# Making the last layers' weights once, ahead of the scans, and loading them for the third batch from another queue

## The chip, the cores and the metric

The kernel runs on one core of one Trainium2 chip. The metric is the device time of one execution in microseconds (us); lower is better. The core's engines run beside each other, each through its own list of instructions in order: TensorE (PE in the profile, PEld for its weight loads), VectorE (DVE), ScalarE (ACT), GpSimd (POOL) and SyncE (SP), which here only issues DMAs. They wait for each other on semaphores. ACT and POOL can issue DMAs too.

## The reference, cut to what matters

The input has four batches of 384 channels by 32 by 32 positions. Two layers follow one another, each a mixer and a feed-forward part with a residual around it:

```python
# layer 0: a selective scan in four directions, then a mixture of experts
x = x + _L0_conv_ref(_ln_c(x), ...)          # scan over 1024 positions, 16 states, 4 directions
t = t + _L0_ffn_ref(_ln_t(t), ...)           # 4 experts, the 2 best for each token
# layer 1: attention with 8 heads, then a feed-forward part with Kronecker weights
x = x + _L1_conv_ref(_ln_c(x), ...)          # out = einsum('bne,ce->bnc', out, w_out) + b_out
t = t + _L1_ffn_ref(_ln_t(t), ...)

def _L1_ffn_ref(x, c_fc_1, c_fc_2, c_proj_1, c_proj_2):
    w_fc = jnp.kron(c_fc_1, c_fc_2)          # (1536, 32) by (1, 12): 1536 by 384
    w_proj = jnp.kron(c_proj_1, c_proj_2)
    h = jax.nn.gelu(x @ w_fc.T, approximate=False)
    return h @ w_proj.T
```

The "last layers" are attention's output projection (`w_out`), the layer norm of tokens behind it, and `_L1_ffn_ref`. The norm's mean can be worked into the first weight (each value of `c_fc_2` less the mean of its row over the 384 columns), and `c_proj_2` into the last one. Both are what the change is about. These weights are the same for all batches.

## The kernel before, in words

**Tiling.** A batch is 384 channels by 1024 positions: three chunks of 128 partitions, two halves of 512 columns. The scans (`scan_layer`) run over 32 units: four batches, four directions, two halves. In each unit `chunk` runs over three chunks of channels and four groups of states. Its work on the engines: POOL multiplies (L445 and L473, `bx`), ACT takes exponentials (L454, `da`), DVE scans (L459) and multiplies (L466), and PE sums over states (L480, `acc`). SP issues the loads of the scan's operands (`dtr` L429, `bcs` L355), which `project` has written to DRAM as `dd` (L410, L411) and `both`.

**The tail of a batch.** When the scan of batch b is done, `between(b)` emits `tail_batch(b - 1)`: the experts of that batch, then attention, then `last_layers`. So a tail is interleaved with the scan of a later batch: the first batch's last layers lie near 1600 us, beside the end of the second batch's scan, and the second batch's near 2550, beside the start of the fourth's. The third batch's lie near 3510, just after all scans, and the fourth's near 4106, with nothing beside them. The fourth batch's experts begin right after the third batch's attention; their weights (`w`, 576 KB each, L927 and L935, loaded by SP in `fetch`) go into a second set of buffers (the `Room` called "w", with ten `kw` buffers) that is free only after the scans.

**Attention** (`attention`) works over four pairs of heads t, two halves i and eight blocks j. PE makes scores (L1146, `s_ps`), ACT their exponentials (L1152, `ex`), and PE the weighted sum (L1195, `o_acc`), which ACT copies to `att` once for each half (L1203). Then `divide` sums the rows on DVE (L1160, `inv`), takes the reciprocal there (L1161), spreads it by PE (L1168, `bc_ps`) and multiplies on DVE (L1173).

**The last layers** (`last_layers`) load three tiles: `wa` (576 KB, three quarters of `w_out`, L1219), `wb` (384 KB: the last quarter of `w_out`, and the mean-free first weight `wz`, L1221) and `wc` (576 KB: `fc1`, `pj1` and `pj2`, L1223). DVE then subtracts the mean from `wz` in place (L1225) and multiplies `pj2` by `c_proj_2` (L1230). PE projects attention's output (L1248, `o_ps`, which takes `wa` and, for the last quarter, `wb`), and so on to the output. All three tiles have the tag `kw`, whose eight buffers (`NARROW`) they share with attention's own tiles and with expert weights.

**What sets the order.** The kernel is one program of tiles without an order written by hand. `build` opens it with `schedule_with_timeline_sim=True`: a planner lays out each engine's list by its own estimate of when operations become ready, with priorities. `last_layers` is emitted under `high_priority(offset=FORWARD)`, so that its operations come ahead of others when they are ready. Operations that need nothing late, such as those of `moe_consts`, are laid out near the start of the kernel, although the code calls them in the first tail. Once laid out, an engine's list is fixed, and an instruction that waits holds everything behind it on its engine.

**The queues.** All loads and stores shown here are issued by SP, except the two first loads (`cols` L128, `wx` L199) and the first gather of each batch's tokens (`xs`, L952, for s equal to 0), which ACT issues, and the scatters and gathers by index (L697, L1044), which POOL issues.

Of the kernel before, what the change touches and what calls it, by code (L numbers as in the profile page):

```python
# [9 lines left out]
F32 = mybir.dt.float32  # L10
I32 = mybir.dt.int32
AF = mybir.ActivationFunctionType
ALU = mybir.AluOpType
# [4 lines left out]
P = 128  # L18
B = 4
D = 384  # L20
# [40 lines left out]
KR = 32  # L61
KJ = D // KR
# [12 lines left out]
COL = {}  # L75
# [42 lines left out]
class Body:  # L118
# [436 lines left out]
    def moe_consts(self, room):  # L555
        nc, a, wp = self.nc, self.a, self.const


        turn = wp.tile([P, DC, P + NE], F32, tag="turn", name="turn")
        wg = turn[:, :, P:]  # L560
        nc.sync.dma_start(out=wg, in_=a["wg"].rearrange("(c p) e -> p c e", p=P))
        for c in range(DC):
            nc.vector.tensor_copy(turn[:, c, :P], self.ident)
        ps = room.bank("p", "wg_ps")
        for c in range(DC):
            nc.tensor.matmul(ps[:, :NE], self.ones, wg[:, c, :], start=(c == 0), stop=(c == DC - 1))
        for c in range(DC):
            nc.vector.scalar_tensor_tensor(
                wg[:, c, :], ps[:, :NE], -1.0 / D, wg[:, c, :], op0=ALU.mult, op1=ALU.add
            )  # L570
        self.turn = turn
        bg = wp.tile([P, NE], F32, tag="bg", name="bg")
        nc.sync.dma_start(out=bg, in_=a["bg"].partition_broadcast(P))
        self.bg = bg

        def count(name, shape, pattern, base=0, channel=0):
            i = wp.tile([P, *shape], I32, tag=name, name=name + "_i")
            nc.gpsimd.iota(i, pattern=pattern, base=base, channel_multiplier=channel)
            f = i.bitcast(F32)
            nc.vector.tensor_copy(f, i)  # L580
            return f


        before = count("before", [P], [[1, P]], channel=-1)
        nc.vector.tensor_scalar(before, before, 0.0, None, op0=ALU.is_gt)
        self.before = before
        lower = count("lower", [NE, NE], [[1, NE], [-1, NE]])
        nc.vector.tensor_scalar(lower, lower, 0.0, None, op0=ALU.is_gt)
        self.lower = lower
        self.full = count("full", [L // P], [[P, L // P]])  # L590
        self.slot_at = count("slot_at", [NSLOT], [[1, NSLOT]])
        self.number = count("number", [MB], [[P, MB]], base=1, channel=1)
        self.column = count("column", [P], [[1, P]], base=1)


        size = NROW
        self.rows = self.dram.tile([size, W], F32, tag="rows", name="rows")
        self.made, self.zeroed, self.taken = [], [], []
        for b in range(B):
            self.made.append(self.dram.tile([STORED, D], F32, tag=f"made{b}", name=f"made{b}"))  # L600
# [607 lines left out]
    def last_layers(self, b, att, room, between=()):  # L1208
# [4 lines left out]
        nc, a = self.nc, self.a  # L1213
        nq = P // KR
        nt = INNER // P


        wa = room.tile([P, nt - 1, D], "kw", "wa")
        nc.sync.dma_start(out=wa, in_=a["wa"].rearrange("p (t d) -> p t d", d=D))  # L1219
        wb = room.tile([P, 2, D], "kw", "wb")  # L1220
        nc.sync.dma_start(out=wb, in_=a["wb"].rearrange("p (t d) -> p t d", d=D))  # L1221
        wc = room.tile([P, 3, D], "kw", "wc")
        nc.sync.dma_start(out=wc, in_=a["wc"].rearrange("p (t d) -> p t d", d=D))  # L1223
        wz = wb[:, 1, :]
        nc.vector.tensor_scalar(wz, wz, self.c2mean, None, op0=ALU.subtract)  # L1225
        fc1 = wc[:, 0, :].rearrange("p (q m) -> p q m", m=P)
        pj1 = wc[:, 1, :].rearrange("p (f r) -> p f r", r=KR)
        pj2 = wc[:, 2, :]
        lo, hi = COL["pj2"]
        nc.vector.tensor_mul(  # L1230
            pj2.rearrange("p (r j) -> p r j", j=KJ), pj2.rearrange("p (r j) -> p r j", j=KJ),
            self.cols[:, lo:hi].unsqueeze(1).to_broadcast([P, KR, KJ]),
        )

        x2 = [room.tile([P, L], "kw", "x2") for _ in range(DC)]
        zt = room.tile([P, NH, HF], "k4", "z")
# [1 line left out]
        for i in range(NH):  # L1238
            part = []
# [3 lines left out]
            for c in range(DC):  # L1243
                ps = room.bank("p", "o_ps")
                chunk = slice(c * P, (c + 1) * P)
                for t in range(nt):
                    w = wa[:, t, chunk] if t < nt - 1 else wb[:, 0, chunk]
# [73 lines left out]
        for i in range(NH):  # L1321
            out = room.bank("p" if between and i == 0 else "o", "f_acc")
# [252 lines left out]
```

## Time and profile before

| | us |
|---|---|
| median of 3 runs | 4209.68 |
| lowest and highest of the runs | 4201.19 and 4214.02 |
| the profiled execution's own time | 4199.62 |
| its span in the profile | 4197.9 |

| engine | busy us | share of the span | instructions |
|---|---|---|---|
| PE | 3348.0 | 80% | 13372 |
| PEld | 1574.9 | 38% | 13372 |
| DVE | 2872.9 | 68% | 4250 |
| ACT | 2463.8 | 59% | 4485 |
| POOL | 3022.8 | 72% | 1476 |

The mean clock granted to TensorE is 0.877 of full speed. The profile is of one execution; times in it count from the start of its span. Busy shares are averages over stages with different limits, so what a change is worth has to be read in its stage: by windows (busy time of each engine between two times), by timelines (the instructions of one engine in order, with the idle time before each and who ended it), and by waits (who waited for whom). A name such as `bx<-dtr,bcs` means that tile `bx` is written from `dtr` and `bcs`. A line such as L445 is a line of the kernel; SPq and ACTq are DMAs that SP and ACT issue, and their length is that of the issue and not of the transfer.

### The profile page before, as it was taken

Reading aid. Unit: us, or ns where it says so; the run is one execution under the profiler, and the core shown is the slowest. Engines: PE = TensorE matmul, PEld = TensorE weight load, DVE = VectorE, ACT = ScalarE, POOL = GpSimd, SP = SyncE. Lnnn points to the kernel's source line nnn. Section 1 sums busy time; section 2 is a strip of 40 time slices with the busy share of each in tenths; the row PEclk is TensorE's granted clock in tenths of the full one; section 3 lists DMA queues with packets and bytes.
Section 4 is the critical chain, followed back from the end, with each engine's and each line's share of the span. In section 5 each row is a group of like instructions: output and inputs, shape, how many; then the busy total and the mean of one; then the engine's idle time right before and its main releaser. Section 6 shows DMA issues by size and latency. Waiting matters only on the chain. (4 is left out here: it accounts for less than half of the span.)

```text
span 4197.9 us, 45862 instructions
## 1 busy us (share of the span) xinstructions
PE 3348.0 (80%) x13372; PEld 1574.9 (38%) x13372; DVE 2872.9 (68%) x4250; ACT 2463.8 (59%) x4485; POOL 3022.8 (72%) x1476
## 2 busy tenths in 40 slices
PE   6545454479987888789996887789996988999899
PEld 2101111145553223255553223245563224577423
DVE  5999997878887877788887867788887862010101
ACT  5555555556665776776665776676665774421353
POOL 5999997898989877798989976888998961000100
PEclk8666666589998999799998998789998999999999
DMA  5554464577986444577886434568887424356200
GB/s 139 126 136 124 111 176 111 154 226 217 254 249 179 103 131 120 170 213 228 233 252 192 112 105 137 153 195 241 224 249 220 109 64 170 122 179 208 88 6 31
DMA packets 378883, 677.67 MB, mean 161 GB/s; under 512 B 49920, under 2 KB 179328, under 8 KB 378624
## 3 DMA queue, kind: packets, MB, share of 16 engines
q1 hardware_dynamic: 368800, 647.42, 54.1%
q0 software_dynamic: 8192, 25.21, 1.9%
q8 instruction: 108, 1.77, 0.2%
q10 hardware_dynamic: 1632, 2.04, 0.2%
q14 instruction: 151, 1.24, 0.1%
HBM read 566.68 MB, written 107.79 MB: 161 GB/s over the span
## 5 line engine op out<-in xcount | busy, mean ns | idle before, releaser
L445 POOL TENSOR_TENSOR bx<-dtr,bcs 128x1024 f32<-128x1024 f32 x768 | 1795.4, 2365 | 189.1 <-PE acc L480 103.1
L454 ACT ACTIVATE da<-dtr,nega 128x512 f32<-128x512 f32 x1536 | 1044.5, 690 | 921.1 <-DVE bx L466 568.3
L473 POOL TENSOR_TENSOR bx<-bx,bcs 128x1024 f32<-128x1024 f32 x384 | 907.2, 2366 | 138.3 <-DVE carry L470 69.2
L480 PE MATMUL acc<-bx,sel 128*32 128x512 f32 x3072 | 495.4, 707 | 320.8 <-POOL bx L473 294.6
L991 PE MATMUL h_ps<-xc,w 128*128 128x256 f32 (+1 forms) x3168 | 652.3, 361 | 45.6 <-DMA w<-in_w 18.4
L1013 PE MATMUL y_ps<-w,hs 128*128 128x384 f32 x1824 | 630.2, 497 | 26.9 <-ACT hs L1004 18.7
L991 PEld LDWEIGHTS h_ps<-xc,w 128*128 128x128 f32 x3168 | 547.4, 196 | 202.4 <-issue 87.0
L459 DVE TENSOR_TENSOR_SCAN bx<-da,carry,bx 128x512 f32<-128x512 f32 x384 | 474.1, 1270 | 118.2 <-POOL bx L445 64.8
L459 DVE TENSOR_TENSOR_SCAN da<-da,carry,bx 128x512 f32<-128x512 f32 x384 | 475.9, 1273 | 77.6 <-ACT da L454 68.7
L459 DVE TENSOR_TENSOR_SCAN bx<-da,bx 128x512 f32<-128x512 f32 x384 | 451.9, 1210 | 95.1 <-POOL bx L445 54.7
L466 DVE TENSOR_TENSOR bx<-da,bcs 128x512 f32<-128x512 f32 x768 | 509.4, 680 | 3.9 <-DMA bcs<-both 0.4
L459 DVE TENSOR_TENSOR_SCAN da<-da,bx 128x512 f32<-128x512 f32 x384 | 455.2, 1218 | 68.8 <-ACT da L454 55.5
L1013 PEld LDWEIGHTS y_ps<-w,hs 128*128 128x128 f32 x1824 | 345.1, 193 | 305.3 <-issue 56.1
L1146 PE MATMUL s_ps<-w 64*128 64x512 f32 x1024 | 311.2, 663 | 76.6 <-ACT ex L1152 72.2
L1152 ACT ACTIVATE ex<-s_ps 128x512 f32<-128x512 f32 x512 | 300.7, 591 | 107.3 <-PE s_ps L1146 105.7
L1044 POOL DMA_INDIRECT got<-made,g_source x64 | 61.2, 957 | 401.1 <-PE h_ps L991 381.4
L999 ACT ACTIVATE hs<-h_ps,bb 128x256 f32<-128x256 f32 (+1 forms) x528 | 200.4, 441 | 240.5 <-PE h_ps L991 178.5
L1195 PE MATMUL o_acc<-ex,vt 128*64 128x512 f32 x1024 | 287.5, 639 | 23.2 <-ACT ex L1152 20.8
L480 PEld LDWEIGHTS acc<-bx,sel 128*32 128x32 f32 x3072 | 73.9, 116 | 611.2 <-POOL bx L473 404.8
L1146 PEld LDWEIGHTS s_ps<-w 64*128 64x128 f32 x1024 | 83.6, 190 | 287.3 <-ACT ex L1152 235.7
L370 PE MATMUL dt_ps<-xd,wdt 108*128 108x512 f32 x192 | 124.7, 736 | 59.5 <-ACT mag L409 30.5
L1017 DVE TENSOR_TENSOR y<-y_ps,bb 128x384 f32<-128x384 f32 x76 | 41.7, 549 | 170.0 <-PE y_ps L1013 170.0
(240 smaller groups left out, 3594.2 us busy)
## 6 DMA issues: line engine op xcount, KB each, us to landing
w<-in_w SPq DMA_DIRECT2D x352, 576.0 KB
dtr<-dd SPq DMA_DIRECT2D x1536, 128.0 KB
bcs<-both SPq DMA_DIRECT2D x512, 128.0 KB
dd<-one_e SPq DMA_DIRECT2D x96, 256.0 KB
dd<-mag SPq DMA_DIRECT2D x96, 256.0 KB
xt<-x SPq DMA_DIRECT2D x32, 384.0 KB
made<-y SPq DMA_DIRECT2D x32, 384.0 KB
xs<-rows SPq DMA_DIRECT2D x28, 385.0 KB
```

Source lines behind the costliest of these rows:

```text
L445: pool = nc.gpsimd.tensor_mul(bx, dtr[q][1], bc[:, 0].unsqueeze(1).to_broadcast([P, 2, HF])).ins
L454: nc.scalar.activation(da, dtr[q][0][:, j, :], AF.Exp, scale=nega[:, col : col + 1])
L459: nc.vector.tensor_tensor_scan(run(h), run(da), run(bx[:, j, :]), 0.0 if first else hold, ALU.mult, ALU.add,)
L466: dve = nc.vector.tensor_mul(bx[:, j, :], h, cg).ins
L473: pool = nc.gpsimd.tensor_mul(bx, bx, cg.unsqueeze(1).to_broadcast([P, 2, HF])).ins
L480: nc.tensor.matmul(acc[lo : lo + DB, :], sel, out[q][:, j, :], start=(g == 0), stop=(g == NG - 1),)
L991: ins = nc.tensor.matmul(ps[:, r, :], w1[(f + r) // wf][:, c, (f + r) % wf * P : ((f + r) % wf + 1) * P], xc[:, c, :], start=(c == 0), sto ...
L999: done = nc.scalar.activation(hs[:, f + r, :], ps[:, r, :], AF.Gelu if last or alone else AF.Identity, bias=bb[:, f + r : f + r + 1],).ins
L1013: nc.tensor.matmul(out[:, :D], hs[:, f, t * P : (t + 1) * P], w2[f // wf][:, f % wf, :], start=(f == 0), stop=(f == FC - 1),)
L1146: ins = nc.tensor.matmul(ps, w[rows, j * P : (j + 1) * P], w[rows, halves(i)], start=True, stop=True).ins
L1152: done.append(nc.scalar.activation(ex[:, o, :], ps, AF.Exp, scale=HD**-0.5, accum_out=sums[:, t, 2 * j + o, i : i + 1],).ins)
L1195: ins = nc.tensor.matmul(out[cols, :], made[t][1][:, j, cols], ex[:, o, :], start=(j == 0), stop=(j == MB - 1),).ins
```

## The change

`wb` and `wc` are no longer loaded raw and finished by DVE in each batch. In `moe_consts` they are loaded once, by ACT's queue, into two `kw` buffers; DVE subtracts the mean and multiplies by `c_proj_2` there; and ACT's queue stores the finished tiles to two tiles in DRAM. `last_layers` loads from those. Its three loads are issued by SP as before in batches 0, 1 and 3, and by ACT in batch 2, the third. The two DVE operations in `last_layers` are gone. `wa` still comes straight from the input.

```diff
@@ moe_consts
+        self.weights = []
+        for name, n in (("wb", 2), ("wc", 3)):
+            w = room.tile([P, n, D], "kw", name)
+            nc.scalar.dma_start(out=w, in_=a[name].rearrange("p (t d) -> p t d", d=D))
+            part = w[:, n - 1, :]
+            if name == "wb":
+                nc.vector.tensor_scalar(part, part, self.c2mean, None, op0=ALU.subtract)
+            else:
+                lo, hi = COL["pj2"]
+                part = part.rearrange("p (r j) -> p r j", j=KJ)
+                nc.vector.tensor_mul(
+                    part, part, self.cols[:, lo:hi].unsqueeze(1).to_broadcast([P, KR, KJ])
+                )
+            ready = self.dram.tile([P, n, D], F32, tag=name, name=name)
+            nc.scalar.dma_start(out=ready, in_=w)
+            self.weights.append(ready)
@@ last_layers
+        queue = nc.scalar if b == B - 2 else nc.sync
         wa = room.tile([P, nt - 1, D], "kw", "wa")
-        nc.sync.dma_start(out=wa, in_=a["wa"].rearrange("p (t d) -> p t d", d=D))
+        queue.dma_start(out=wa, in_=a["wa"].rearrange("p (t d) -> p t d", d=D))
         wb = room.tile([P, 2, D], "kw", "wb")
-        nc.sync.dma_start(out=wb, in_=a["wb"].rearrange("p (t d) -> p t d", d=D))
+        queue.dma_start(out=wb, in_=self.weights[0])
         wc = room.tile([P, 3, D], "kw", "wc")
-        nc.sync.dma_start(out=wc, in_=a["wc"].rearrange("p (t d) -> p t d", d=D))
+        queue.dma_start(out=wc, in_=self.weights[1])
         wz = wb[:, 1, :]
-        nc.vector.tensor_scalar(wz, wz, self.c2mean, None, op0=ALU.subtract)
...
-        lo, hi = COL["pj2"]
-        nc.vector.tensor_mul(
-            pj2.rearrange("p (r j) -> p r j", j=KJ), pj2.rearrange("p (r j) -> p r j", j=KJ),
-            self.cols[:, lo:hi].unsqueeze(1).to_broadcast([P, KR, KJ]),
-        )
```

## The prediction

> **What bounds the kernel now.** I read the table of slices, then windows by stage, then what waits inside the stages that the edit touches (timelines of one engine each, and the queue's waits). Windows first; columns are stretch, length, then PE, PEld, DVE, ACT, POOL busy (instructions), granted clock, DMA share, GB/s.
>
> ```profile
> 1640.10:1798.60 158.50, 119.68 (x414) 45.38 (x413) 111.16 (x238) 106.34 (x159) 121.02 (x68) 0.80 0.53 158
> 2545.20:2702.00 156.80, 118.10 (x444) 48.73 (x442) 113.77 (x231) 90.93 (x164) 108.23 (x63) 0.83 0.51 157
> ...
> 2702.00:3428.00 726.00, 627.07 (x2629) 317.54 (x2631) 597.62 (x809) 490.69 (x851) 653.99 (x311) 0.91 0.67 187
> ...
> 3522.00:3900.00 378.00, 378.00 (x1576) 256.73 (x1575) 34.62 (x65) 104.91 (x192) 6.70 (x7) 0.99 0.49 160
> ```
>
> During the scans (44 to 3428 us) POOL is the fullest engine, 654 of 726 in the third row, with DVE just behind and feeding it. The exceptions are the first units of a batch's scan: in the first unit of the fourth batch (second row) POOL works 108.2 of 156.8. From 3522 to 3900 TensorE is full. So a stop of DVE counts in the scans, a stop of PE counts after them. The last layers stand in both.
>
> The second batch's DVE and POOL timelines (start, length, engine, line, operation, idle before and who ended it):
>
> ```profile
> 2545.14 0.27 DVE L470 COPY carry<-bx 128x1 f32<-128x1 f32 x2
> 2549.86 10.64 DVE L1225 TENSOR_SCALAR wb<-wb,c2mean 128x384 f32<-128x384 f32 x1 [4.45 <-DMA wb<-in_wb]
> 2560.42 2.33 DVE L459 TENSOR_TENSOR_SCAN da<-da,bx 128x512 f32<-128x512 f32 x2
> ```
> ```profile
> 2551.03 9.26 POOL L445 TENSOR_TENSOR bx<-dtr,bcs 128x1024 f32<-128x1024 f32 x4
> 2568.89 2.34 POOL L473 TENSOR_TENSOR bx<-bx,bcs 128x1024 f32<-128x1024 f32 x1 [8.61 <-DVE carry L470]
> 2576.69 2.35 POOL L473 TENSOR_TENSOR bx<-bx,bcs 128x1024 f32<-128x1024 f32 x1 [5.45 <-DVE carry L470]
> ```
>
> An operation that takes 0.41 us when POOL is idle (fourth batch, 4073.43) stood 10.64 us here, until POOL's row of products ended at 2560.3; with the wait for its weights before it, DVE did nothing else for 15.1 us. POOL ran ahead on its buffers, then stood 8.6 and 5.5 us.
>
> The third batch, PE, then DVE, then SP's queue:
>
> ```profile
> 3509.11 1.08 PE L1195 MATMUL o_acc<-ex,vt 128*64 128x512 f32 x4 [0.34 <-ACT ex L1152]
> 3521.79 2.39 PE L1168 MATMUL bc_ps<-ident,inv 128*64 128x128 f32 x18 [11.60 <-DVE inv L1161]
> ```
> ```profile
> 3520.97 0.42 DVE L1225 TENSOR_SCALAR wb<-wb,c2mean 128x384 f32<-128x384 f32 x1 [11.69 <-DMA wb<-in_wb]
> 3521.50 0.24 DVE L1161 RECIPROCAL inv<-inv 128x16 f32<-128x16 f32 x1
> ```
> ```profile
> 3493.21 3.69 SPq L935 DMA_DIRECT2D w<-in_w  x4
> 3499.49 4.78 SPq L927 DMA_DIRECT2D w<-in_w  x2
> 3505.60 0.35 SPq L1219 DMA_DIRECT2D wa<-in_wa  x1
> 3508.43 2.69 SPq L1221 DMA_DIRECT2D wb<-in_wb  x1
> 3511.25 0.35 SPq L1223 DMA_DIRECT2D wc<-in_wc  x1
> ```
> ```profile
> SPq L1219 <- DMA w<-in_w: 1.3, 1, 1.3
> ```
>
> PE idles 11.6 us because the reciprocal is queued on DVE behind L1225, which waits for wb, which SP issued behind ten loads of expert weights. The last row matters too: the load of wa waited for an earlier load to land. The operands in the trace show eight completion semaphores that DMAs of SP and ACT take in turn, so each load waits until the load eight before it has landed. SP could go on at 3505.6, 3508.4 and 3511.2.
>
> **The change, part by part.** The sum is made against the profiled execution, 4199.6 us, 10.1 under the median 4209.7.
>
> Removed in all: four L1225 (13.3 us busy, 22.2 idle before) and four L1230 (2.6 and 0.5), 38.6 us of DVE. That is the ceiling without the queue's move; what counts is less.
>
> First batch: DVE stood from 1595.8 to 1603.7, but its next scan needs a product that POOL ended at 1601.2. Gain 2.4 us, plus some of L1230's 0.9: 2.5 (0 to 4).
>
> Second batch: the next scan's product (L445, 2545.16, 2.37 us) was ready at 2547.5, and the scan began at 2560.4: 12.9 us. POOL's two stalls behind it sum to 14.1, and ACT waited 12.9 in one piece for DVE. I take 12.5 (4 to 15). The Trainium skill speaks here, in "SBUF — State Buffer", section "Who interferes with whom": DVE's two-port modes and GpSimd exclude each other, and whoever issues first holds the port pair for that instruction. By it L1225 loses at most the POOL product under way, 2.4 us, so the stop would be 4.5 + 2.4 + 0.4 = 7.3 and the gain some 5. The row shows four and a half products passing first. The row is used; by the rule the sum below would be 7.5 us worse.
>
> Third batch, DVE: PE's 11.6 us wait for the reciprocal goes, less the 0.5 that the reduction and the reciprocal take themselves: gain 11.1. Next late would be wa (landed 3519) for o_ps, if it stayed on SP.
>
> Third batch, the queue: three loads leave SP and stand in ACT's order. In the first two batches they are issued within 3 us of ACT's copy of the last att tile's first half (copies at 1597.4 and 2546.4); in the third that copy is at 3494.47, between exponentials, and SP got there late. I place them on ACT right behind it. There they need the same landings of expert weights, so ACT stands until 3505.6, 3508.4 and 3511.2 and is free at 3511.6. Queued behind are 14 exponentials, which PE's o_acc and the end of attention wait for. Between 3495.1 and 3510.2 the before did 15.1 us of that work; it would now end at 3526.7: cost 16.5. Bounds: 0, if the loads land in free semaphores, to 17. Issues cost three times 0.37, contained in this. ACT's own xs<-rows (3514.98) moves back to some 3527; PE wants it at xc_ps, 3539.7 before and 5 later then, and that load took under 8 us, so it is hidden. SP gets its xt loads (3517.2) about as before, since their buffers wait for these exponentials. POOL's scatters (L697) are done by 3508.
>
> On the move the skill's "DMA: Bandwidth & Descriptors", section "Issuing engines are not separate DMA queues", says that another issuing engine saves only the issue time, since all run on the same 16 engines. By it the move gains 0.4 us an issue and the stop costs its 16.5 in full. The row has wb landing 12.5 us after its issue with four big loads ahead on SP, so landing earlier is worth something, but only to 3511.
>
> Third batch together: -11.1 + 16.5 = +5.4. PE is full for 378 us afterwards, so this passes to the end whole.
>
> Fourth batch: L1225 and L1230 (0.41, 0.55) run beside a full PE, 30 us before o_ps needs them: 0. Were PE not full they would cost 1.
>
> Ahead of the scans: two more loads (384 and 576 KB), two DVE operations (0.42 and 0.55, POOL idle), two stores, all on ACT's queue. ACT is idle from 4.9 to 11.9, DVE from 5.2 to 11.1. They share the DMA engines with the first half of u (768 KB, landed 5.6); at some 250 GB/s (1216 KB in 5 us) 384 KB more beside it is 1.5 us. The stores' wait for DVE stands ahead of ACT's L177 at 11.9; if wc lands after 11 us, layernorm slips. I take 1.5 (0 to 5).
>
> Sum: +1.5 - 2.5 - 12.5 + 5.4 = -8.1, so 4191.5 for this execution and 4201.6 for the median.
>
> **Rivals.**
> A, the sum: 4201.6, with 4190 to 4213 around it from its bounds.
> B, ACT does not stand: the loads come ahead of the expert fetches in the order, or behind the last exponential. For it: only 5 us separate the first fetch (3489.4) from the copy. Against: fetches wait for nothing but the router, and ACT stood 3.6 us on DMA semaphores ahead of its own load (L952, 3511.3 to 3514.9). Then 4209.7 + 1.5 - 2.5 - 12.5 - 11.1 = 4185.1.
> C, slower: the order of all engines is written by the planner from its own times, and six operations fewer on DVE, four DMAs more and three on another queue rewrite it. Place: first units of the batches. POOL idles 18.2 us in the second batch's (757.1 to 885.4), 37.5 and 48.6 in the next two, for the same scan work. A new order may cost one unit the 19.3 between the first two, or two units 38.6; the middle, 29, gives 4230.6. It decides from 20.7 us of added idle (8.1 + 12.6).
> D, the DVE stop is replaced: scan and POOL meet their next limit at once, so the second batch gives 2 and the first 1. 4209.7 + 1.5 - 3 + 5.4 = 4213.6. Against it: ACT and POOL both name DVE as releaser.
> That the change doesn't do what it says I leave out: both DVE lines go, and nothing recomputes them.
>
> **How the numbers follow.** A 0.40, B 0.28, C 0.20, D 0.12. 0.3% is 12.6 us, about what a measurement of this kernel can tell (its three runs span 12.8). Faster: B, and 0.3 of A: 0.40. Same: 0.68 of A and 0.85 of D: 0.37. Slower: C and the rest: 0.23. A and B lie on one side and hold most; their own range is 4180 to 4213. For eight in ten the low end takes B with the upper gains of batches one and two (4 and 15 instead of 2.5 and 12.5, and 0 ahead of the scans: 4180, and 4 more of order): 4176. The high end takes most of C: 4228.
>
> **What would show it.** No DVE row on wb or wc in any scan; the gap before L459 at 2560 gone and POOL's idle in that unit down from 48.6 to about 36. ACT in the third batch: three ACTq issues behind the copy of att and a hole of about 16 us among the exponentials; bc_ps follows its reciprocal without the 11.6. If that hole is not there, B. First ln_mean at about 7 instead of 5.6. Wrong if POOL's idle in the fourth batch's first unit stays, or if units far from the last layers change by over 5 us each: then the order did it.

## The result: 0.23% slower, and where its trace loses and gains

| kernel | median us (runs) | lowest to highest | ratio to before, 95% interval |
|---|---|---|---|
| before | 4205.2 (15) | 4194.6 to 4214.1 | |
| changed | 4215.4 (15) | 4208.1 to 4220.0 | 1.0023, 1.0015 to 1.0032 |
| changed, run again later (e7) | 4212.4 (12) | 4204.9 to 4220.0 | 1.0016, 1.0005 to 1.0026 |

The forecast was 4201.6, in a range from 4176 to 4228. The time lies in the range and on the other side of before.

To see where the time goes, both traces are divided at the end of each scan unit (the end of its last POOL product, L473). Lengths in us:

| stretch | before | changed | difference |
|---|---|---|---|
| unit 0, with what lies ahead of the scans | 137.5 | 138.0 | +0.5 |
| units 1 to 14 | 1378.8 | 1378.7 | -0.1 |
| unit 15 (the first batch's last layers) | 123.9 | 121.7 | -2.2 |
| unit 16 | 158.5 | 168.1 | +9.6 |
| units 17 to 23 | 746.6 | 748.3 | +1.7 |
| unit 24 (the second batch's last layers) | 156.8 | 141.5 | -15.3 |
| units 25 to 31 (the rest of the fourth batch's scan) | 725.8 | 740.2 | +14.4 |
| after the scans | 770.1 | 776.1 | +6.0 |

So the stop of DVE in the second batch went as forecast, and the seven units behind it gave nearly all of it back. Two windows of the changed kernel, in the columns of those before (unit 24, and units 25 to 31):

```profile
2554.80:2696.30 141.50, 117.65 (x454) 49.26 (x454) 104.50 (x230) 91.23 (x164) 109.77 (x63) 0.87 0.60 179
2696.30:3436.50 740.20, 627.18 (x2631) 317.43 (x2631) 597.01 (x807) 493.01 (x856) 653.02 (x309) 0.92 0.64 182
```

In unit 24 POOL's idle time fell from 48.6 to 31.7. In the second row every engine does the work that it did before (POOL 653.0 against 654.0), in 14.4 us more: nothing was added there, the engines wait longer.

The second batch's last layers in the changed kernel, DVE and then POOL:

```profile
2554.68 0.27 DVE L470 COPY carry<-bx 128x1 f32<-128x1 f32 x2
2557.12 2.35 DVE L459 TENSOR_TENSOR_SCAN da<-da,bx 128x512 f32<-128x512 f32 x2 [2.17 <-POOL bx L445]
```
```profile
2560.58 9.35 POOL L445 TENSOR_TENSOR bx<-dtr,bcs 128x1024 f32<-128x1024 f32 x4
2569.87 2.37 POOL L473 TENSOR_TENSOR bx<-bx,bcs 128x1024 f32<-128x1024 f32 x1
2574.48 2.35 POOL L473 TENSOR_TENSOR bx<-bx,bcs 128x1024 f32<-128x1024 f32 x1 [2.24 <-DVE carry L470]
```

The carry is followed by the next scan after 2.2 us, where 15 us of waiting and standing lay. POOL no longer idles ahead of the first L473 product behind its row of four, and 2.2 us ahead of the next (8.6 and 5.5 in before).

What POOL waits for in units 25 to 31 (us in total, times, longest), before and then changed:

```profile
POOL bx L473 <- DVE bx L459: 23.0, 11, 6.7
POOL bx L445 <- PE acc L480: 12.0, 8, 2.7
POOL bx L473 <- DVE carry L470: 6.6, 5, 3.4
```
```profile
POOL bx L473 <- DVE bx L459: 27.7, 12, 7.3
POOL bx L445 <- PE acc L480: 22.3, 11, 4.9
POOL bx L473 <- DVE carry L470: 15.2, 10, 4.1
```

These are the scan's own hand-overs (DVE's product, PE's sum that frees a buffer, DVE's carry). Together they take 23.6 us more and POOL's other waits some 8 less, as its idle time in the units grew by 15 (87.2 against 72.0). From 2564 us (ACT and PE) to 2581 us (SP) of the before on, the two programs issue their operations in different orders on every engine; up to there the order is the same but for the lines of the diff.

The third batch, ACT and then PE, in the changed kernel:

```profile
3507.00 0.60 ACT L1169 ACTIVATE ex<-s_ps 128x512 f32<-128x512 f32 x1 [0.30 <-PE o_acc L1212]
3511.99 0.59 ACT L1220 COPY att<-o_acc 128x512 f32<-128x512 f32 x1 [4.31 <-remote]
3512.00 0.35 ACTq L1237 DMA_DIRECT2D wa<-in_wa  x1
3514.63 0.34 ACTq L1239 DMA_DIRECT2D wb<-wb  x1
3522.50 0.33 ACTq L1241 DMA_DIRECT2D wc<-wc  x1
3522.87 0.60 ACT L1169 ACTIVATE ex<-s_ps 128x512 f32<-128x512 f32 x1 [10.29 <-remote]
```
```profile
3512.63 1.98 PE L1212 MATMUL o_acc<-ex,vt 128*64 128x512 f32 x4 [4.59 <-issue]
3523.61 2.08 PE L1163 MATMUL s_ps<-w 64*128 64x512 f32 x4 [9.00 <-ACT ex L1169]
```

The three loads stand right behind the copy of `att`, as forecast, and no exponential runs between 3507.6 and 3522.9. PE's 11.6 us for the reciprocal are gone; it idles twice in attention instead. (The 4.3 us ahead of the copy belong to a slowed stretch like the one described next, not to the loads.)

**Unit 16 is another matter.** Its program is in the same order in both kernels. What differs is one stretch, here ACT in the changed kernel and then in e1, where all of this is the same program too:

```profile
1742.55 0.59 ACT L1327 COPY hs<-h_ps 128x512 f32<-128x512 f32 x1 [2.01 <-remote]
1745.37 0.59 ACT L1327 COPY hs<-h_ps 128x512 f32<-128x512 f32 x1 [2.23 <-PE h_ps L1321]
1750.96 0.59 ACT L1327 COPY hs<-h_ps 128x512 f32<-128x512 f32 x1 [5.01 <-remote]
```
```profile
1749.76 1.07 ACT L1327 COPY hs<-h_ps 128x512 f32<-128x512 f32 x2 [1.67 <-PE h_ps L1321]
```

SP's small steps (registers, checks) follow each other every 0.70 us or twice that there, 0.02 to 0.3 otherwise. The traces of the changed kernel and of e5 to e8 (which ran together, on one chip) have such a stretch; those of before, of e1 to e4 and of e9 to e12 have none. So it goes with where or when a kernel ran and not with the change. The 9.6 us of unit 16 in the table are therefore no cost of the change, and lengths of unit 16, and of attention after the scans, are compared below only between traces that agree in it, or with a word on it. Ratios are always to runs of before that were taken beside the kernel's own.

### The profile page after: what moved, and what is told of

It reads as the page before. It is cut to its first block, busy times and chain, and to the rows that moved or that the text cites. A ratio compares the mean times of both kernels' runs of the same rounds, so it can differ in the third digit from the quotient of the medians.

```text
span 4212.6 us, 45855 instructions
## 1 busy us (share of the span) xinstructions
PE 3340.4 (79%) x13372; PEld 1574.9 (37%) x13372; DVE 2859.7 (68%) x4244; ACT 2468.5 (59%) x4487; POOL 3023.2 (72%) x1476
## 5 line engine op out<-in xcount | busy, mean ns | idle before, releaser
L473 POOL TENSOR_TENSOR bx<-bx,bcs 128x1024 f32<-128x1024 f32 x384 | 906.4, 2365 | 140.9 <-DVE carry L470 65.6
```

The costliest lines, as they stand in the source:

```text
L473: pool = nc.gpsimd.tensor_mul(bx, bx, cg.unsqueeze(1).to_broadcast([P, 2, HF])).ins
```

## The experiments

All were run against before, with 8 to 22 runs of each changed program and 31 to 56 of before; e1 to e4, e5 to e8 and e9 to e12 ran on one chip each. "Queue" means which engine issues the third batch's three loads.

**e1: the change without the queue's move.**

```diff
-        queue = nc.scalar if b == B - 2 else nc.sync
+        queue = nc.sync
```

> The changed kernel with one thing undone: the third batch's three loads are issued by SP, as in the other batches. Every engine's order is that of the changed kernel but for these three issues. Theory S (ACT's stand): in the changed kernel ACT does nothing between 3508.1 and 3522.9 but issue these loads; without them attention's last exponentials run through and, as DVE has no stop on wb left, the wait of PE for the reciprocal (11.6 us before) does not come back. The third batch then gains 8.6 (what it lost against before) and 11.1: 4215.4 - 19.7 = 4195.7. Rival M (memory): the loads compete with expert weights whoever issues them; wa lands at about 3527 (3519 before, and the scans end 8.6 later), o_ps waits for it, and most of the 11.1 is lost: 4204 to 4212. The stretch of 9.6 us lost in the unit after 1640 does not depend on this edit: if it comes from the program it is in this trace too, if it belonged to one execution it is not.

Measured: 1.0000 of before (0.9991 to 1.0010). Rival M's size, not S's: PE waits for `wa` in place of the reciprocal, 5.04 us here, and the stretch after the scans is only 2.3 us shorter than in before (767.8). Unit 16 took 159.9. Unit 24 took 140.1, units 25 to 31 took 743.0. Against the changed kernel, the queue's move costs 0.16 to 0.23%.

**e2: before, with the queue's move alone** (`queue` as in the change, weights raw, DVE's lines kept).

> The kernel before, with only the queue moved: the third batch loads wa, wb and wc raw by ScalarE's queue, DVE still subtracts and multiplies. The order of the scans is that of before. Theory S: ACT stands some 15 us among attention's last exponentials and DVE still waits for wb, both in the same stretch, so the stand sets the end: between +3 and +6, 4208 to 4211. Rival: the loads come earlier than by SP (wb landed 12.5 us after its issue there), DVE's stop ends earlier, and the time falls by up to 5: 4200 or more. If the stand is only there because this execution of the changed kernel had SP and ACT slowed between 3507 and 3514, the trace shows the three issues without the first 4.3 us.

Measured: 1.0016 (1.0008 to 1.0023), which is +6.7 us of 4192, a little over the 3 to 6 of theory S. PE, in attention:

```profile
3509.41 2.08 PE L1146 MATMUL s_ps<-w 64*128 64x512 f32 x4 [15.47 <-ACT ex L1152]
```

This trace has no slowed stretch, and PE's hole is 15.5 us all the same (ACT's own idle time is 16.04). The stretch after the scans grew by 3.6 only (773.7), since PE's 11.6 us for the reciprocal are not in this trace: the loads landed during the stand.

**e3: all loads by SP, and the second batch raw and finished on DVE as before.**

```diff
-        queue.dma_start(out=wb, in_=self.weights[0])
+        raw = b in (1,)
+        if raw: ...   # load and finish as in the kernel before
```

> The changed kernel with two things undone: all loads by SP, and the second batch loads wb and wc raw and finishes them on DVE as before. The order of every engine in the scans is then that of the kernel before. Theory O (order): the first batch gives 3 and the third its 11.1 (PE's wait for the reciprocal), the start costs 0.5: 4205.2 - 13.6 = 4191.6, and the units of the fourth batch's scan are each within 2 us of before. Rival M: o_ps waits for wa instead, third batch gives 3: 4200. If the 9.6 us lost in the unit after 1640 come from the program (its order there is the same in this kernel), they are here too, and the time is 4201 by O.

Measured: 0.9979 (0.9970 to 0.9988), between the 0.9968 of O and the 0.9988 of M; the trace tells them apart. After the scans 770.0 us, as before (770.1): the 11.1 us that were forecast for the reciprocal's wait are not gained at all. PE, and SP's queue:

```profile
3506.80 3.78 PE L1274 MATMUL o_ps<-att,wa 128*128 128x512 f32 x4 [9.38 <-DMA wa<-in_wa]
```
```profile
3492.32 0.35 SPq L1237 DMA_DIRECT2D wa<-in_wa  x1
```

This is M. Units 25 to 31, in the order of before: 725.1. That the trace is shorter anyhow comes mostly from unit 24 (146.9): the same operation on the same data as before stood 2.20 us behind POOL, not 10.64. DVE, then POOL:

```profile
2545.24 2.20 DVE L1254 TENSOR_SCALAR wb<-wb,c2mean 128x384 f32<-128x384 f32 x1 [3.68 <-DMA wb<-in_wb]
```
```profile
2544.83 2.40 POOL L473 TENSOR_TENSOR bx<-bx,bcs 128x1024 f32<-128x1024 f32 x1
2547.16 9.75 POOL L445 TENSOR_TENSOR bx<-dtr,bcs 128x1024 f32<-128x1024 f32 x4
```

DVE was done at 2547.4, as the L473 product ended, and POOL's row of four came after it.

**e4: all by SP, wb prepared everywhere, wc raw in the second batch.** (The same edit as e3, for `wc` alone.)

> The changed kernel with all loads by SP, and in the second batch wc alone loaded raw and multiplied on DVE; wb is prepared in all batches. So DVE's long stop on wb is gone in the second batch too (15 us), but the order of all engines in the fourth batch's scan stays that of the kernel before. Theory O: the stop's 15 us are kept to the end, as nothing is reordered: 15 below e3, about 4177. Rival N (elastic): the scan gives the gain back in its next units whatever the order, since POOL and the loads meet their own limits there: the end of the scans is within 4 us of e3's, about 4190. The difference between e1 and this kernel is then what the new order costs: 14 to 19 by O, under 5 by N.

Measured: 0.9987 (0.9980 to 0.9995), 1.7 us over e3. It is N's number, but not by N's mechanism. Units 25 to 31 took 722.4; nothing was given back there. The gain was never made, as the multiply took over the stop (DVE, unit 24):

```profile
2542.97 9.54 DVE L1264 TENSOR_TENSOR wc<-wc,cols 128x384 f32<-128x384 f32 x1
```

Both theories had left that out, so the run says nothing between them.

**e5: all prepared, all by SP, the order of before.**

```diff
+        if b == 1:
+            nc.vector.tensor_reduce(self.idle, pj2, AX.X, ALU.add)
```

> The changed kernel with all loads by SP and, in the second batch alone, one reduction of pj2 into an unused column on DVE (it reads one operand and its result is used nowhere). With it the planner lays out PE, ACT, POOL and the scans' SP order as in the kernel before, and wb and wc are prepared in all batches. Theory O (the new order of the fourth batch's scan costs what the stop's removal gives): no stop on DVE is left in the second batch, unless the reduction too stands behind POOL's run; e3 still lost 3.7 + 2.2 + 1.5 there and e4 9.5, so 6 to 8 below e3 and e4, ratio to before 0.9965, about 4178; against e1, the same work in the new order, 12 to 18 less. Rival N (the scan gives it back in its next units whatever the order): within 2 of e3 and e4. If the reduction stands 5 to 10 us behind POOL, this run tells nothing on O, and shows that one operand is enough to be locked out.

Measured: 0.9967 (0.9954 to 0.9980); expected by O 0.9965. Unit 24 took 144.3, units 25 to 31 took 728.1. N is refuted: with the order kept the gain stays. Against e1 that is 0.33%, 14 us, for the same work in another order. The order of PE's and POOL's operations in this trace is that of before without an exception. (The two intervals leave the 14 us uncertain by about half; e11 gives a second pair.)

**e6: e5 with the third batch's loads ahead of the fourth batch's first expert weights on SP.**

```diff
-        weights, xc = fetch(0), gather(0)
+        with self.tc.issue_after(self.last_load) if alone else nullcontext():
+            weights = fetch(0)
+        xc = gather(0)
```

> e5, and SP's order changed at one place: the first fetch of the fourth batch's expert weights (ten loads) is queued behind the third batch's wa, wb and wc, not ahead of them. Theory M (o_ps waits 9.4 us for wa since SP reached it behind ten loads of 576 KB): wa lands before attention ends, the wait goes, and the experts, 60 us later on PE, still find their weights: 9 below e5. Rival P (POOL's scatters): the three loads also wait for scatters whose buffers they take (wb 3.1 us in e3), which end some 85 us after the scans, so only 3 to 5 of the 9.4 go. Rival E (expert weights late): they start 22 us later, and PE waits at h_ps; then the time is that of e5 or worse.

Measured: 0.9960 (0.9947 to 0.9973), the lowest of all, though not resolved from e5. In the traces of e5 and e6 the slowed stretch lies over attention's end (after the scans 773.0 and 773.3), the loads land behind it in both, and PE waits for `wa` in neither, so the run does not decide between its theories. e12 gives the answer.

**e7: the changed kernel again.**

> The changed kernel itself once more, beside the others on this chip. If the 9.6 us that its trace lost in the unit after 1640 (same order on all engines as before, SP's steps 0.70 us apart instead of 0.05) belong to one execution, this trace does not have them there. ACT's stand at the third batch's loads should be there again, 11 to 16 us. Ratio to before 1.0023 as measured, and 7 to 10 us over e1.

Measured: 1.0016. Unit 16 has the slowed stretch again (166.9), and so have e5, e6 and e8 beside it (167.7, 169.9, 168.9): so it is not one execution's, and not this change's. Units 25 to 31 took 748.7. PE's hole at the three loads was 16.48 us. Against e5 on the same chip it is 0.49% slower: order and queue together (0.33 and 0.16).

**e8: before with the preparation ahead of the scans alone.**

> The kernel before with only the preparation ahead of the scans (two loads, two DVE operations, two stores on ACT's queue); nobody reads the stored tiles, and all batches load raw and finish on DVE as before. Every other instruction keeps its place. By the prediction's term +1.5 (0 to 5). Rival: the shift moves when DVE meets POOL's runs in the second batch, and the time falls by up to 8 as in e3, where the stop took 5.9 instead of 15.1.

Measured: 0.9990 (0.9977 to 1.0004). Unit 0 ended 0.6 us later than in before, which is less than the scatter: in the kernels with this preparation it took 134.4 to 139.2 us. The stop in unit 24 was 3.4 us of waiting and 2.51 of standing, and the unit took 147.4, as the rival had it in the trace; the ratio tells neither from no change, and whether the runs without a profile were lucky in the same way can't be seen.

**e9: e1 with wb raw in the second batch: the new order, with the stop.** (As e3, for `wb` alone.)

> e1 (the changed kernel, all loads by SP) with wb alone loaded raw in the second batch and its mean subtracted there on DVE, as before. The order of the fourth batch's scan is the changed kernel's, but the stop is back. Theory O: the new order by itself costs 0.33% (e1 1.0000 against e5 0.9967), so this kernel stands as far over e3 (0.9979, same operations but for one multiply, order of before): ratio to before 1.000 to 1.003, and units 25 to 31 together take 735 to 750 us in the trace against 725 in the order of before. Rival N: the units after the second batch's last layers only give back what was gained, and with the stop there is nothing to give back: they take 725 to 730, ratio 0.998.

Measured: 1.0012 (0.9997 to 1.0027). O. The stop is back (unit 24: 154.8), and units 25 to 31 took 741.6 although there was no gain to give back:

```profile
2545.05 11.54 DVE L1258 TENSOR_SCALAR wb<-wb,c2mean 128x384 f32<-128x384 f32 x1 [3.56 <-DMA wb<-in_wb]
```

**e10: e1 with one harmless multiply that makes the planner choose a third order.**

```diff
+        if b == 1:
+            ps = room.bank("p", "idle_ps")
+            nc.vector.tensor_mul(ps[:, 0:D], pj2, self.ones[:, 0:1].to_broadcast([P, D]))
```

> e1 with one multiply more in the second batch's last layers: DVE writes pj2 to a PSUM bank that nobody reads. It makes the planner lay out a third order of the fourth batch's scan, with over a thousand places different from both others on PE alone. It has the wait for wc[...]. Theory O: the time of units 25 to 31 depends on the order, so it comes out different from both 725 and 743 by more than 3, in either direction; total between 0.995 and 1.004 of before. Rival N: 740 to 745 again, ratio 1.000, as the gain is given back in any order.

Measured: 1.0004 (0.9996 to 1.0013). Units 25 to 31 took 737.5, with single units quite unlike both others (110.3 us for unit 26, 98.9 before; 141.8 for unit 29, 135.6 before). The 737.5 lie 5.5 us under e1's 743.0, as O said, but only 2.7 under the changed kernel's 740.2. The single units tell the third order from the new one; the time alone would not.

**e11: e5 with the queue's move.** (`queue` as in the change.)

> e5 (order kept, no stop) with the third batch's loads by ScalarE's queue, as in the changed kernel. If the parts add up: e5's 0.9967 and the 0.0016 of the queue alone (e2): 0.9983. If the queue only hurts where the order is new too, or where DVE still waits for wb: 0.9967.

Measured: 0.9988 (0.9977 to 0.9998); the parts add up. After the scans 776.0 us, against 770.0 in e3, and neither trace has a slowed stretch; PE's hole in attention was 16.54 us. The changed kernel, with the same queue and the same work in the new order, measured 1.0023 and 1.0016: 0.28 to 0.35% more, so this pair gives the order the same price as e5 and e1.

**e12: before with the loads first.** (The edit of e6, and nothing else; the planner also moves eight of PE's matmuls near 3534 us.)

> The kernel before with one thing changed: the first fetch of the fourth batch's expert weights is queued behind the third batch's wa, wb and wc on SP. Weights stay raw, DVE finishes them. Theory M: the third batch's end hangs on when the three loads land and not on DVE's two operations; with the loads ahead of 576 KB times ten, PE's 11.6 us wait for the reciprocal shrinks to 0 to 4 and nothing else grows: 0.9975 to 0.9985 of before. Rival P: the loads wait for POOL's scatters, and where SP and ACT are slowed at that place (as in e5 to e8), attention itself ends 12 us later and covers the loads: 0.9995 to 1.0005.

Measured: 0.9986 (0.9975 to 0.9997); after the scans 763.6 us, 6.5 less than before. Theory M. PE:

```profile
3504.45 1.25 PE L1170 MATMUL bc_ps<-ident,inv 128*64 128x128 f32 x18
3505.63 2.84 PE L1250 MATMUL o_ps<-att,wa 128*128 128x512 f32 x6
3519.66 4.57 PE L1252 MATMUL o_ps<-ident,xt 128*128 128x128 f32 x24 [2.25 <-DMA xt<-x]
```

`bc_ps` and `o_ps` follow attention without a wait, though DVE still finishes raw weights: SP issued `wa` at 3489.1, not 3505.6. Only the residual's load `xt` is now 2.25 us late.

## Why the prediction was wrong, step by step

**Lengths side by side.** All traces, us:

| | unit 24 | units 25 to 31 |
|---|---|---|
| order of before, stop of 9.5 us or more: before, e2, e4 | 156.8, 155.4, 152.6 | 725.8, 725.5, 722.4 |
| order of before, short stop: e3, e8, e12 | 146.9, 147.4, 147.1 | 725.1, 728.1, 728.0 |
| order of before, no stop: e5, e6, e11 | 144.3, 145.1, 140.6 | 728.1, 725.9, 725.4 |
| new order, stop of 11.5: e9 | 154.8 | 741.6 |
| new order, no stop: changed, e1, e7 | 141.5, 140.1, 145.4 | 740.2, 743.0, 748.7 |
| third order, no stop: e10 | 144.6 | 737.5 |

The first column goes by the stop, whatever the order; the second goes by the order, whatever the stop. Each length is of one trace, but the traces come from several chips and lie close: 722.4 to 728.1 in the order of before, 740.2 to 748.7 in the new one.

**The step that failed** is the sum, which put the new order of the fourth batch's scan at nothing: it took the scan's seven other units to run as before. Rival C named the mechanism and got 0.20. Its place was wrong: not the first units of batches, whose idle time fell, but units 25, 28 and 30 (+5.7, +7.2 and +16.5 in the changed kernel; unit 29 gave 9.9 back). Its price of 29 was too high: units 25 to 31 take 14 to 23 us more, and by runs 14 (e1 against e5). Put on the sum of -8.1 that gives some +6 to +15, and the runs show +7 to +10: slower, but short of the 20.7 from which C was to decide. The prediction's own test, units far from the last layers that change by over 5 us each, was met by units 28, 29 and 30 (unit 25, next to them, changed by 5.7). Without the order's price the sum was near: e11 has all the rest of the change and measures 0.12% under before, some 5 us, where 8.1 were forecast.

**Ahead of the scans:** forecast +1.5, measured +0.5 in the trace (first `ln_mean` at 6.08 instead of 5.64, not 7) and +0.6 in e8, both within the scatter of unit 0.

**First batch:** forecast -2.5, measured -2.2.

**Second batch:** forecast -12.5, measured -15.3 in unit 24, and -12 to -16 from before to e5, e6 and e11. That the row's figure came true was luck in part, for the row was one draw. DVE's subtraction stood 10.64, 10.88 and 11.54 us in before, e2 and e9, and 2.20, 2.51 and 1.09 in e3, e8 and e12. In all six traces it became ready during the same POOL instruction, the L473 product ahead of the row of four. In e3, e8 and e12 it was done as that product ended. This is what the Trainium skill says in "SBUF — State Buffer", section "Who interferes with whom": between a DVE instruction in a two-port mode and a GpSimd one, whichever issues first holds the shared port pair for that instruction, and the other waits. The stop with the wait ahead of it was 5.9 us in each, where the prediction worked out 7.3 from that page. In the other three POOL went on with its row, and DVE stood to the end of it. The moment of arrival does not tell the two apart: 0.27, 0.96 and 1.15 us into the product for the long ones, 0.11, 0.41 and 1.51 for the short ones. What decides it stays open.

**Third batch:** forecast +5.4, measured +6.0 in the changed kernel, whose attention has a slowed stretch, and +6.0 in e11, which has none. The terms were right as they were put together and would have misled one by one. ACT's stand left PE a hole of 15.5 to 16.5 us in e2, e7 and e11 (forecast 16.5). The 11.1 us of the reciprocal's wait are gained only if the loads land early too: left on SP, `o_ps` waits 9.4 us for `wa`, so the DVE lines alone are worth 0.1 us there (e3), and 2.3 to 5.6 in the new and the third order (767.8 in e1, 764.5 in e9, 767.4 in e10). The prediction named that next wait and did not use it for rival B, whose 4185.1 counts the 11.1 in full. B's premise is also out: the three issues came right behind the copy.

**The sum by runs:** preparing the weights with the order kept -0.33% (e5), the new order +0.33% (e1 against e5), the queue +0.16% (e2): +0.16%, and the changed kernel has +0.16 and +0.23%. That the sum fits to a hundredth is chance, as each part is known to about 0.1. Rival D (the stop replaced by the next limit at once) is refuted by e5.

Which exchange of instructions makes the new order slower was not tried. What is shown is that the order as a whole costs it, with the same work.

## What to carry to other kernels

Where a planner lays out the order, an edit has two effects, the work and the new order. Separate them by an idle instruction of like cost that keeps the order: here each was worth about 14 us, with opposite signs, and the better kernel (e6, 0.40% under before) lay one idle reduction and one ordering of loads away. When a wait is taken away, look up when the next operand in that row lands before counting the gain. And loads that may have to wait for landings should not be queued on an engine that still has work to feed TensorE: here that cost 0.16% (e2).

## What the runs showed of the hardware that I had not expected

Finishing the weights on DVE (a subtraction in place, or a product with a second tensor in SBUF) sometimes stood to the end of POOL's row of four products: 10.64, 10.88 and 11.54 us for the subtraction (before, e2, e9) and 9.54 for the product (e4), where each takes 0.41 and 0.55 beside an idle POOL. In all other cases these operations stood 2.53 us at most, to the end of the POOL instruction under way, even where such a row went on: in e3 the product with `cols` stood 1.52 us and was let in between the second and the third of the four. So passing over the waiting DVE is not the rule, and no run shows what brings it about. A reduction that reads one tensor did not stand in any of its three traces (0.55 us in each). In e11 (DVE, then POOL):

```profile
2542.68 0.55 DVE L1248 TENSOR_REDUCE idle<-wc 128x1 f32<-128x384 f32 x1 [0.52 <-DMA wc<-wc]
```
```profile
2542.03 9.32 POOL L446 TENSOR_TENSOR bx<-dtr,bcs 128x1024 f32<-128x1024 f32 x4
```

The slowed stretches came where SP fetches expert weights while POOL scatters tokens, near 840, 1745 or 3500 us, in the changed kernel's trace and all four of e5 to e8, and in none of before, e1 to e4 and e9 to e12. A full DMA alone is not the cause: its share at 835 to 855 us is 1.03 in e7, which is slowed there, and 1.03 in e1, which is not. The median of before was 4205.9 beside e5 to e8, 4192.3 beside e1 to e4 and 4190.0 beside e9 to e12. Unit 16 is some 9 us longer in them, and after the scans about 3 (773 against 770 in the order of before). What makes the difference stays open.
